# Bounds check for empty places, and one score product for two heads, in a transformer block with mixture of experts

## Chip, cores and metric

The kernel runs on one core of a Trainium2 chip. The metric is device time in microseconds. Three runs of the kernel before gave 1973.52, 1975.29 and 1976.34 us; their median is 1975.29 us.

## What is computed

Sixteen sequences of 512 tokens with 256 features pass a block in fp32. First comes windowed attention: 16 heads of 16 features, windows of 64 queries, which see the band of the 64 keys up to their own. It is mixed by a gate with a linear state-space scan, and an MLP (256 to 1024 to 256) follows. Then each token goes to the two best of 8 experts. The core of the reference:

```python
scores = jnp.einsum('bhncd,bhnkd->bhnck', Qb, Kw) / np.sqrt(Dh)
p = jax.nn.softmax(jnp.where(mask, scores, -jnp.inf), axis=-1)
o = jnp.einsum('bhnck,bhnkd->bhncd', p, Vw)
...
x = x + g * attn + (1.0 - g) * y_ssm
x = x + jax.nn.gelu(h @ mlp_W1 + mlp_b1, approximate=False) @ mlp_W2 + mlp_b2
...
weights, sel = jax.lax.top_k(xf @ gate_w, k=2)
y = experts(xf)                     # swiglu, 8 experts, 256 -> 512 -> 256
out = (take(y, sel) * softmax(weights)).sum()
x = x + gb * out
```

## The kernel before

**Two stages.** Stage one handles a sequence ("batch") at a time: `front` (layer norms, products for q, k and v, scan, gate), `attention` (four tiles of 128 queries), `back` (MLP) and `route` (choice of experts). Stage two, `experts`, handles tiles of 256 places, each of one expert: 64 whole tiles, then 3 half tiles of 128 places.

**The order.** Each part is a generator that yields due times, in units of a batch. The constants in lines 38 to 69 hold them (for example `SCORES`, `VALUES`, `TURNS` for attention and `FULL` for the experts). The loop at the end (lines 1189 to 1194) always advances the part that is due first, and `InOrder` (line 182) makes each engine keep the order in which instructions were written. So batches overlap, and the first expert tiles overlap with the last batch. A different constant moves an instruction on its engine's queue.

**Scores.** A product contracts over 32 partitions, which hold two heads of 16 features. To keep the two apart, `front` (lines 611 to 626) stores q twice, with the features of one head of each pair set to zero by the factors `par`. It copies from PSUM with DVE into copy 0 and with ACT into copy 1; k is copied once, by ACT. `scores` (line 681) then makes 32 products for 128 queries: 2 feature halves, 2 copies, 2 windows, 4 row groups, each 64 queries by 128 keys. In the trace each product is two matmul instructions, so 64 for a tile. `masked`, `numerators` and `turn` add the mask, take the exponent and transpose; `values` (line 732) multiplies by v, in two halves (`chunk`) of 16 products into the PSUM tile `po`.

**Places.** `route` gives each of a token's two choices a row in the DRAM table `place_d`: the token's number and its weight. `place` (line 892) writes 128 rows with an indirect DMA from POOL; a small memset of `between` separates two writes in a row. Each expert has `CAP` rows. Rows that get no token have weight zero, but still need a row of the output to which a tile's scatter-add can add zero, and which no other place of that tile writes. So the table gives them numbers of tokens that did not choose this expert: `others` (line 906) works these out from batch 0, and `fill` (line 924) writes them with 32 more indirect DMAs, from due time 3.5 on, one every 6 us of due time.

**An expert tile.** `places_of` (line 264) loads the tile's rows and also the rows one tile before (`mt`, two blocks). `gather` (line 280) casts the token numbers (`gi`), gathers the tokens from `h_d` (`hr`), and works out the output row `si` on POOL: the tile's own token where the weight is positive, else the other block's. `turned`, `hidden` and `combine` transpose, run the expert, and add the result to the output by an indirect DMA that accumulates. A scatter-add waits until both of the previous tile's have landed, and the cast into a buffer of `si` waits until the scatter-add that last used it has landed.

Of the kernel before, what the change touches and what calls it, by code (L numbers as in the profile page):

```python
# [8 lines left out]
F32 = mybir.dt.float32  # L9
# [28 lines left out]
FRONT = (-1.4961, -1.0671)  # L38
XT = -0.6
QK = (-0.5602, -0.4769, -0.4522, -0.3053)  # L40
V = (-0.0188, 0.0729)
DRIVE = 0.1154
GATE = (-0.0778, 0.205)
BACK = (1.1529, 1.2977)
UP = (
    (1.4542, 1.4907, 1.5377, 1.6049),
    (1.6857, 1.7521, 1.7795, 1.9017),
)
GELU = (1.6239, 2.022)
DOWN = (  # L50
    (1.7436, 1.7759, 1.8584, 2.12),
    (2.1788, 2.1889, 2.2678, 2.288),
)
ROUTE = 2.3576
RATE = 0.01396

LOGITS_GAP = -1.6691
TOKENS_GAP = 1.9608

FULL = (15.9711, 16.4769, 16.5285, 16.7838, 0.0292)  # L60

SCORES = -0.9527
MASKED = (-0.9009, -0.6206)
NUMERATORS = (-0.5391, -0.2136)
NUMERATORS_EACH = 0.1267
TURNS = (0.3291, 0.6595)
OVER_SUMS = 0.8221
VALUES = (1.1056, 1.1201)
MIX = 1.5924
# [6 lines left out]
CAP = TS + TOKENS  # L76
# [8 lines left out]
NROW = NE * CAP + (NE + 1) * TS  # L85
# [3 lines left out]
def block_kernel(  # L89
# [72 lines left out]
    for e in range(NE):  # L162
        nc.gpsimd.memset(rev[:, :, e], float(NE - e))
        nc.gpsimd.memset(first_place[:, :, e], float(e * CAP + TS))

# [8 lines left out]

    idle = w.tile([P, NE + 1, 2, 2], F32, name="idle")
    nc.vector.memset(idle, 0.0)
    nc.gpsimd.iota(
        idle[:, :, :, 0], pattern=[[0, NE + 1], [1, 2]], base=0, channel_multiplier=2,
        allow_small_or_imprecise_dtypes=True,
    )  # L180

# [82 lines left out]
    def places_of(room, j):  # L264

        n = parts(j)
        r = register(room["rows"](j), NROW - 2 * n * P)
        mt = room["mt"]([P, 2, n, 2], F32, name=f"mt_{j}")
        last_load[:] = [
            nc.sync.dma_start(  # L270
                out=mt,
                in_=place_d[bass.ds(r, 2 * n * P), :].rearrange("(q p h) c -> p q h c", p=P, h=n),
            )
        ]
        if j in (0, FIRST):
            for put in placed:
                tc.add_manual_dep(last_load[0].ins, put.ins.name, landed)
        return mt

    def gather(room, j, mt):  # L280

        before, mt = mt[:, 0], mt[:, 1]
# [137 lines left out]
    with ExitStack() as p1, ExitStack() as p2:  # L420
# [17 lines left out]
        cT_sb = load(cT, "cT_sb")  # L438
# [28 lines left out]
        sc = w1p.tile([P, KC, NB], F32, name="sc")  # L467
# [22 lines left out]
        for half in range(2):  # L490
# [30 lines left out]
        prefill += [  # L521
            nc.sync.dma_start(
                out=place_d[: NE * CAP, :].rearrange("(p r) c -> p (r c)", p=P),
                in_=v_cross.rearrange("p t h e -> p (t h e)")[:, : NE * CAP * 2 // P],
            ),
            nc.sync.dma_start(
                out=place_d[NE * CAP :, :].rearrange("(q p h) c -> p q h c", p=P, h=2), in_=idle
            ),
        ]
# [52 lines left out]
        def front(b, t):  # L582
# [28 lines left out]
            t["q"] = q = sb.tile([P, 2, KC, SEQ], F32, tag="q", name=f"q_{b}")  # L611
            t["k"] = kT = sb.tile([P, KC, WIN + SEQ], F32, tag="k", name=f"k_{b}")
            gpsimd.memset(kT[:, :, 0:WIN], 0.0)
            for c in range(2 * KC):
# [66 lines left out]
        def scores(b, t, qt):  # L681
# [6 lines left out]
            for c in range(KC):  # L688
                for e in range(2):
                    for half in range(2):  # L690
                        n = 2 * qt + half
                        for j in range(4):
                            rs = slice(32 * j, 32 * j + 32)
                            tensor.matmul(
                                sc[j // 2][half * WIN : (half + 1) * WIN, j % 2, 2 * c + e, :],
                                q[rs, e, c, n * WIN : (n + 1) * WIN],
                                kT[rs, c, n * WIN : (n + 2) * WIN],
                                start=True, stop=True,
                            )
# [192 lines left out]
        def place(row, at, **kwargs):  # L892

            if placed and gpsimd.last is placed[-1]:
# [3 lines left out]
                in_=row, in_offset=None, **kwargs,  # L898
            )
            for zeros in prefill:  # L900
                tc.add_manual_dep(put.ins, zeros.ins.name, landed)
# [3 lines left out]

        def others(both, pr):

            far = float(NROW)
            nr = few.tile([P, NT, NE], F32, tag="nr", bufs=1, name="nr")
            vector.tensor_sub(nr, tok0[:, :NT].unsqueeze(2).to_broadcast([P, NT, NE]), pr)  # L910

            over = few.tile([P, NT, NE], F32, tag="over", bufs=1, name="over")
            vector.tensor_single_scalar(over, nr, float(TS), ALU.is_ge)
            vector.tensor_max(over, over, both)
            vector.tensor_add(nr, nr, first_place)
            vector.scalar_tensor_tensor(nr, over, far, nr, ALU.mult, ALU.add)
            ni = few.tile([P, NT, NE], I32, tag="ni", bufs=1, name="ni")
            vector.tensor_scalar_add(ni, nr, -float(TS))
            none = few.tile([P, NT, 2], F32, tag="none", bufs=1, name="none")
            gpsimd.memset(none, 0.0)  # L920
            gpsimd.tensor_copy(none[:, :, 0], tok0[:, :NT])
            spare.update(none=none, ni=ni)

        def fill(b, t):

            for e in range(NE):
                for i in range(NT):
                    place(
                        spare["none"][:, i, :], spare["ni"][:, i, e : e + 1],
                        bounds_check=NROW - 1, oob_is_err=False,  # L930
                    )
                    yield 6.0

        def route(b, t):
# [77 lines left out]
            if b == 0:  # L1012
                others(both, pr)
# [73 lines left out]
        def last_table():  # L1087

            assert len(routed) == NB and len(placed) == NT * (NE + 2 * NB)
# [12 lines left out]
            vector.tensor_scalar(start[:, :1], whole[:, :1], float(TS), float(P), ALU.mult, ALU.add)  # L1102
# [26 lines left out]
        def experts(_, t):  # L1129
# [5 lines left out]
            assert len(placed) >= NT * (NE + 2 * done)  # L1135
# [23 lines left out]
            for kind, bufs in (  # L1159
                ("w1", 3), ("w2", 3), ("b1", 3), ("b2", 3), ("mt", FIRST + 4), ("gi", 5),  # L1160
                ("real", 5), ("so", 5), ("si", 5), ("hr", 5), ("hT2", 2), ("act", 2), ("g2", 2),
# [17 lines left out]
        spare = {}  # L1179
# [88 lines left out]
```

## Time and profile before

| | |
|---|---|
| runs, median of 3 | 1975.29 us |
| profiled execution | 1981.67 us |
| its span, first to last instruction | 1979.9 us |
| mean granted clock of TensorE | 0.986 |
| busy PE / weight loads / DVE / ACT / POOL | 95% / 78% / 72% / 49% / 61% |
| score products (`sc`) | 4096 instructions, 81.6 us busy |
| products with v (`po`) | 4096 instructions, 111 us busy |
| scatter-adds (`out<-y,si`) | 131, 1685 ns each on POOL |
| place writes / fill writes | 128 / 32, 1035 / 1040 ns each on POOL |

PE is TensorE's matmul queue, PEld its weight loads, which overlap the matmuls, DVE is VectorE, ACT ScalarE, POOL GpSimd, SP SyncE. Most instructions show line 190, the wrapper `InOrder`, so groups are read by the names of their tiles. Stage one lasts until about 1170 us and stage two until the end, with an overlap of some 150 us. The profiled execution is one run, and stands 6.4 us over the median.

### The profile page before, as it was taken

How to read it: one execution, taken by the hardware profiler on the slowest of the kernel's cores; microseconds unless marked ns; L12 is line 12 of the kernel's file. 1: busy time of each engine (PE TensorE's matmuls, PEld its weight loads, DVE VectorE, ACT ScalarE, POOL GpSimd, SP SyncE). 2: the span in 40 equal slices, each digit the busy share in tenths (PEclk: the TensorE clock that was granted, in tenths of full speed). 3: DMA queues.
4: the chain of work that ended last, by engine and by line, in shares of the span. 5: the costliest groups of instructions: out<-in, count | busy, mean ns of one | idle time of the engine just before them, and what ended most of it. 6: DMA issues, size and time to landing. Idle time of an engine off the chain costs nothing.

```text
span 1979.9 us, 45068 instructions
## 1 busy us (share of the span) xinstructions
PE 1877.9 (95%) x16802; PEld 1543.0 (78%) x16802; DVE 1426.1 (72%) x3243; ACT 975.9 (49%) x2880; POOL 1202.8 (61%) x1869
## 2 busy tenths in 40 slices
PE   5889999989999999999999987989999999999996
PEld 2668877767778778877877776878888888888885
DVE  6778888778889888888888764556665656566664
ACT  2877776766777777787777652111111111111110
POOL 2326558667558547646655555757676666666653
PEclk9999999999999999999999998999999999999998
DMA  5202222212222212223122127578887877878774
GB/s 159 79 25 57 66 52 58 66 52 58 60 58 58 71 47 73 55 57 76 52 50 52 42 57 195 139 192 235 230 237 228 241 223 233 238 225 244 222 227 113
DMA packets 148098, 242.76 MB, mean 123 GB/s; under 512 B 46000, under 2 KB 112432, under 8 KB 139040
## 3 DMA queue, kind: packets, MB, share of 16 engines
q1 hardware_dynamic: 113120, 187.32, 32.8%
q0 software_dynamic: 34464, 51.69, 10.9%
q8 instruction: 134, 2.20, 0.5%
q14 instruction: 92, 0.75, 0.2%
q10 hardware_dynamic: 288, 0.79, 0.1%
HBM read 190.27 MB, written 43.19 MB: 118 GB/s over the span
## 4 chain that ended last, share of the span: by engine, by line
PE 73%; ACT 7%; POOL 6%; DVE 6%; issue 4%; DMA 2%; SPq 0%; POOLq 0%; DVEq 0%; ACTq 0%
PE pgv L190 21%; PE pye L190 11%; PE py L190 9%; PE pmlp L190 7%; PE po L190 4%; PE pq L190 4%; PE pp L190 4%; PE sc L190 2%; PE pa L190 2%; ACT sm L190 2%; DMA out<-y,si 2%; PE pv L190 2%; PE pg L190 2%; ACT L190 2%; POOL h L190 2%
## 5 line engine op out<-in xcount | busy, mean ns | idle before, releaser
L190 PE MATMUL pgv<-hT,we 128*128 128x256 f32 (+1 forms) x2144 | 469.1, 377 | 2.9 <-ACT hT L190 2.9
L190 PEld LDWEIGHTS pgv<-hT,we 128*128 128x128 f32 x2144 | 402.9, 192 | 57.6 <-ACT hT L190 3.7
L190 ACT ACTIVATE sm<-sm,nm 128x128 f32<-128x128 f32 x1024 | 399.1, 394 | 3.7 <-DVE nm L190 3.3
L190 DVE TENSOR_SCALAR gv<-pgv,be 128x256 f32<-128x256 f32 (+1 forms) x536 | 230.9, 473 | 182.1 <-PE pgv L190 145.6
L190 ACT ACTIVATE gv<-gv 128x512 f32<-128x512 f32 (+1 forms) x134 | 83.1, 620 | 455.1 <-DVE gv L190 433.3
L190 POOL DMA_INDIRECT out<-y,si x131 | 220.8, 1685 | 109.4 <-DVE y L190 70.1
L190 PE MATMUL pye<-we,act 128*128 128x256 f32 x1048 | 249.8, 382 | 0.5 <-DVE act L190 0.5
L190 PE MATMUL pmlp<-hT,mw_sb 128*128 128x256 f32 x1024 | 246.2, 385 | 0.4 <-ACT hT L190 0.4
L190 PE MATMUL py<-mw_sb,m 128*128 128x256 f32 x1024 | 236.9, 382 | 0.1
L190 PEld LDWEIGHTS pmlp<-hT,mw_sb 128*128 128x128 f32 x1024 | 190.5, 192 | 37.5 <-issue 9.8
L190 PEld LDWEIGHTS pye<-we,act 128*128 128x128 f32 x1048 | 195.3, 192 | 24.9 <-DVE act L190 0.9
L190 PEld LDWEIGHTS py<-mw_sb,m 128*128 128x128 f32 x1024 | 189.8, 190 | 28.5 <-issue 3.2
L190 ACT ACTIVATION_READ_ACCUMULATOR sm<-sm,nm 128x1 f32 x1024 | 195.8, 191 | 0.0
L190 POOL DMA_INDIRECT place_d<-pl,slot x128 | 132.5, 1035 | 100.6 <-DVE pick L190 71.8
L190 POOL TENSOR_TENSOR e<-e,g 128x256 f32<-128x256 f32 x64 | 47.5, 742 | 221.7 <-DVE e L190 221.7
L190 DVE TENSOR_TENSOR sm<-sc,mask 128x1024 f32<-128x1024 f32 x128 | 155.1, 1212 | 16.7 <-PE sc L190 13.2
L190 DVE TENSOR_REDUCE nm<-sm 128x8 f32<-128x1024 f32 x128 | 156.2, 1220 | 4.4
L190 POOL DMA_INDIRECT hr<-h_d,gi x131 | 134.5, 1027 | 38.5 <-issue 19.5
L190 ACT COPY pT<-pp 128x1024 f32<-128x1024 f32 x128 | 128.9, 1007 | 32.3 <-PE pp L190 28.8
L190 PE MATMUL pp<-ident,sm 128*128 128x128 f32 x1024 | 134.8, 275 | 6.9 <-DVE sm L190 6.9
L190 DVE TENSOR_SCALAR m<-pmlp,b_sb 128x256 f32<-128x256 f32 x256 | 109.7, 470 | 40.2 <-PE pmlp L190 38.3
L190 PEld LDWEIGHTS pp<-ident,sm 128*128 128x128 f32 x1024 | 119.3, 143 | 16.1 <-issue 5.7
(219 smaller groups left out, 3217.1 us busy)
## 6 DMA issues: line engine op xcount, KB each, us to landing
we<-in_e_w SPq DMA_DIRECT2D x67, 1024.0 KB
we<-in_e_w SPq DMA_DIRECT2D x67, 512.0 KB
v_cross<-v_own SPq DMA_DIRECT2D x48, 256.0 KB
be<-in_e_b SPq DMA_DIRECT2D x67, 128.0 KB
x<-in_x SPq DMA_DIRECT2D x16, 512.0 KB
xr<-in_x SPq DMA_DIRECT2D x32, 256.0 KB
out<-h SPq DMA_DIRECT2D x16, 512.0 KB
h_d<-hn SPq DMA_DIRECT2D x16, 512.0 KB
```

The source lines that it names most:

```text
L190: put = getattr(self.engine, name)(*args, **kwargs)
```

## The change

Two edits, and new due times.

Places without a token: a place's row is now just token number and weight, and an empty row is all zeros. In `gather` an empty place's output row gets the number of tokens (`TOKENS`) added, so it lies beyond the end of the output, and the scatter-add has a bounds check that drops such rows. `others`, `fill`, `idle` and the second block of `mt` are gone; the table has no spare block ahead of each expert.

Scores: q is stored once, k twice (copy 0 by DVE, copy 1 by ACT). One product now has the 128 keys of both copies side by side, so 16 products of 64 by 256 replace 32 of 64 by 128.

The due times are all new. On the engines' queues this puts the first half of each tile's products with v (16 of `po`) ahead of the scores two tiles on, where before only one tile of four was so split, `pq_3` one MLP product earlier, and in the overlap of the stages the first `prank` ahead of the first expert tile's transpose, and the last batch's `ahead` on POOL behind a scatter-add of tile 2 (before: behind the index casts and scatter-adds of later tiles).

```diff
-SCORES = -0.9527
-MASKED = (-0.9009, -0.6206)
...
-VALUES = (1.1056, 1.1201)
+SCORES = -0.9284
+MASKED = (-0.9272, -0.6892)
...
+VALUES = (1.0622, 1.1426)
-FULL = (15.9711, 16.4769, 16.5285, 16.7838, 0.0292)
+FULL = (15.9709, 16.4684, 16.5007, 17.0256, 0.0287)
...
-CAP = TS + TOKENS
+CAP = TOKENS
-NROW = NE * CAP + (NE + 1) * TS
+NROW = NE * CAP + NE * TS
...
-        mt = room["mt"]([P, 2, n, 2], F32, name=f"mt_{j}")
+        mt = room["mt"]([P, n, 2], F32, name=f"mt_{j}")
...
-        real = room["real"]([P, n], F32, name=f"real_{j}")
-        gpsimd.tensor_single_scalar(real, mt[:, :, 1], 0.0, ALU.is_gt)
+        si = room["si"]([P, n], I32, name=f"si_{j}")
         so = room["so"]([P, n], F32, name=f"so_{j}")
-        gpsimd.tensor_sub(so, mt[:, :, 0], before[:, :, 0])
-        gpsimd.tensor_mul(so, so, real)
-        si = room["si"]([P, n], I32, name=f"si_{j}")
-        gpsimd.tensor_add(so, so, before[:, :, 0])
+        gpsimd.tensor_scalar(so, mt[:, :, 1], 0.0, float(TOKENS), ALU.is_le, ALU.mult)
+        gpsimd.tensor_add(so, so, mt[:, :, 0])
         gpsimd.tensor_copy(si, so)
...
             in_=y, in_offset=None, compute_op=ALU.add,
+            bounds_check=room["tokens"](j) - 1, oob_is_err=False,
...
                 if c < KC:
-                    vector.tensor_scalar_mul(q[:, 0, c, :], pq, par[:, 0:1])
-                    scalar.activation(q[:, 1, c, :], pq, AF.Identity, scale=par[:, 1:2])
+                    scalar.copy(q[:, c, :], pq)
                 else:
-                    scalar.copy(kT[:, c - KC, WIN:], pq)
+                    vector.tensor_scalar_mul(kT[:, c - KC, 0, WIN:], pq, par[:, 0:1])
+                    scalar.activation(
+                        kT[:, c - KC, 1, WIN:], pq, AF.Identity, scale=par[:, 1:2]
+                    )
...
-                for e in range(2):
-                    for half in range(2):
...
-                                sc[j // 2][half * WIN : (half + 1) * WIN, j % 2, 2 * c + e, :],
-                                q[rs, e, c, n * WIN : (n + 1) * WIN],
-                                kT[rs, c, n * WIN : (n + 2) * WIN],
...
+                            sc[j // 2][
+                                half * WIN : (half + 1) * WIN, j % 2, 2 * c : 2 * c + 2, :
+                            ],
+                            q[rs, c, n * WIN : (n + 1) * WIN],
+                            kT[rs, c, :, n * WIN : (n + 2) * WIN],
...
-        def others(both, pr):
-        def fill(b, t):
...
-            if b == 0:
-                others(both, pr)
...
-            (3.5, -1, places(fill(0, {}), 0, 3.5)),
```

More of the change, by code (lines that the diff above doesn't have):

```diff
@@ L34 @@
 NEG = -1.0e30
[L38 to L44, printed above, removed]
+FRONT = (-1.4781, -1.0684)
+XT = -0.6004
+QK = (-0.5706, -0.4649, -0.4626, -0.324)
+V = (-0.0324, 0.0643)
+DRIVE = 0.1113
+GATE = (-0.004, 0.2002)
+BACK = (1.1554, 1.3131)
 UP = (
-    (1.4542, 1.4907, 1.5377, 1.6049),
-    (1.6857, 1.7521, 1.7795, 1.9017),
+    (1.4542, 1.4907, 1.5377, 1.6035),
+    (1.6843, 1.7508, 1.7782, 1.9466),
 )
-GELU = (1.6239, 2.022)
+GELU = (1.6378, 2.0259)
 DOWN = (
-    (1.7436, 1.7759, 1.8584, 2.12),
-    (2.1788, 2.1889, 2.2678, 2.288),
+    (1.7089, 1.8492, 1.8707, 2.1323),
+    (2.1911, 2.2012, 2.2773, 2.2985),
 )
-ROUTE = 2.3576
+ROUTE = 2.3589
 RATE = 0.01396
-LOGITS_GAP = -1.6691
-TOKENS_GAP = 1.9608
-FULL = (15.9711, 16.4769, 16.5285, 16.7838, 0.0292)
-SCORES = -0.9527
-MASKED = (-0.9009, -0.6206)
[L64 to L67, printed above, removed]
-VALUES = (1.1056, 1.1201)
-MIX = 1.5924
+LOGITS_GAP = -1.9886
+TOKENS_GAP = 1.9209
+FULL = (15.9709, 16.4684, 16.5007, 17.0256, 0.0287)
+SCORES = -0.9284
+MASKED = (-0.9272, -0.6892)
+NUMERATORS = (-0.5869, -0.2654)
+NUMERATORS_EACH = 0.1497
+TURNS = (0.4019, 0.6275)
+OVER_SUMS = 0.8312
+VALUES = (1.0622, 1.1426)
+MIX = 1.5922
 TS = 256
@@ L163, in block_kernel @@
         nc.gpsimd.memset(rev[:, :, e], float(NE - e))
-        nc.gpsimd.memset(first_place[:, :, e], float(e * CAP + TS))
+        nc.gpsimd.memset(first_place[:, :, e], float(e * CAP))
     taken = w.tile([P, NE + 1], F32, name="taken")
@@ L173, in block_kernel @@
     nc.vector.memset(gate_sb, 0.0)
[L175 to L180, printed above, removed]
     class InOrder:
@@ L266, in places_of @@
         n = parts(j)
-        r = register(room["rows"](j), NROW - 2 * n * P)
-        mt = room["mt"]([P, 2, n, 2], F32, name=f"mt_{j}")
+        r = register(room["rows"](j), NROW - n * P)
+        mt = room["mt"]([P, n, 2], F32, name=f"mt_{j}")
         last_load[:] = [
@@ L271, in places_of @@
                 out=mt,
-                in_=place_d[bass.ds(r, 2 * n * P), :].rearrange("(q p h) c -> p q h c", p=P, h=n),
+                in_=place_d[bass.ds(r, n * P), :].rearrange("(p h) c -> p h c", h=n),
             )
@@ L280, in gather @@
     def gather(room, j, mt):
-        before, mt = mt[:, 0], mt[:, 1]
         n = parts(j)
@@ L435, in load @@
             return t
-        cT_sb = load(cT, "cT_sb")
+        cT_sb = sb.tile(list(cT.shape), F32, tag="e", bufs=1, name="cT_sb")
+        nc.sync.dma_start(out=cT_sb, in_=cT)
         wm = [
@@ L463, in block_kernel @@
         mw2_sb = w2p.tile(list(mw2.shape), F32, name="mw2_sb")
-        sc = w1p.tile([P, KC, NB], F32, name="sc")
+        sc = sb.tile([P, KC, NB], F32, tag="oT", name="sc")
         nc.scalar.activation(sc, cT_sb, AF.Tanh, scale=0.5)
@@ L520, in block_kernel @@
         nc.gpsimd.memset(v_cross, 0.0)
-        prefill += [
+        prefill.append(
             nc.sync.dma_start(
[L523 to L529, printed above, removed]
+                out=place_d.rearrange("(p r) c -> p (r c)", p=P),
+                in_=v_cross.rearrange("p t h e -> p (t h e)")[:, : NROW * 2 // P],
+            )
+        )
         par = w1p.tile([P, 2], F32, name="par")
@@ L609, in front @@
             yield from to_features(xn, xnT, 0, 0, b)
-            t["q"] = q = sb.tile([P, 2, KC, SEQ], F32, tag="q", name=f"q_{b}")
-            t["k"] = kT = sb.tile([P, KC, WIN + SEQ], F32, tag="k", name=f"k_{b}")
-            gpsimd.memset(kT[:, :, 0:WIN], 0.0)
+            t["q"] = q = sb.tile([P, KC, SEQ], F32, tag="q", name=f"q_{b}")
+            t["k"] = kT = sb.tile([P, KC, 2, WIN + SEQ], F32, tag="k", name=f"k_{b}")
+            gpsimd.memset(kT[:, :, :, 0:WIN], 0.0)
             for c in range(2 * KC):
@@ L622, in front @@
                 if c < KC:
-                    vector.tensor_scalar_mul(q[:, 0, c, :], pq, par[:, 0:1])
-                    scalar.activation(q[:, 1, c, :], pq, AF.Identity, scale=par[:, 1:2])
-                else:
-                    scalar.copy(kT[:, c - KC, WIN:], pq)
+                    scalar.copy(q[:, c, :], pq)
+                else:
+                    vector.tensor_scalar_mul(kT[:, c - KC, 0, WIN:], pq, par[:, 0:1])
+                    scalar.activation(
+                        kT[:, c - KC, 1, WIN:], pq, AF.Identity, scale=par[:, 1:2]
+                    )
             for i in range(0, NT, 2):
@@ L688, in scores @@
             for c in range(KC):
-                for e in range(2):
-                    for half in range(2):
[L691 to L694, printed above, removed]
-                                sc[j // 2][half * WIN : (half + 1) * WIN, j % 2, 2 * c + e, :],
-                                q[rs, e, c, n * WIN : (n + 1) * WIN],
-                                kT[rs, c, n * WIN : (n + 2) * WIN],
-                                start=True, stop=True,
-                            )
+                for half in range(2):
+                    n = 2 * qt + half
+                    for j in range(4):
+                        rs = slice(32 * j, 32 * j + 32)
+                        tensor.matmul(
+                            sc[j // 2][
[3 more added lines that the diff above has]
+                            kT[rs, c, :, n * WIN : (n + 2) * WIN],
+                            start=True, stop=True,
+                        )
             return sc
@@ L890, in one_hot, with place @@
             return mx, oh
-        def place(row, at, **kwargs):
+        def place(row, at):
             if placed and gpsimd.last is placed[-1]:
@@ L897, in place @@
                 out=place_d, out_offset=bass.IndirectOffsetOnAxis(ap=at, axis=0),
-                in_=row, in_offset=None, **kwargs,
+                in_=row, in_offset=None,
             )
-            for zeros in prefill:
-                tc.add_manual_dep(put.ins, zeros.ins.name, landed)
+            tc.add_manual_dep(put.ins, prefill[0].ins.name, landed)
             if placed:
@@ L904, in place @@
             placed.append(put)
-        def others(both, pr):
[L908 to L922, printed above, removed]
-        def fill(b, t):
[L926 to L932, printed above, removed]
         def route(b, t):
@@ L1087, in last_table @@
         def last_table():
-            assert len(routed) == NB and len(placed) == NT * (NE + 2 * NB)
+            assert len(routed) == NB and len(placed) == NT * 2 * NB
             one = room["one"]
@@ L1101, in last_table @@
             start = one.tile([P, 2], F32, name="start")
-            vector.tensor_scalar(start[:, :1], whole[:, :1], float(TS), float(P), ALU.mult, ALU.add)
+            vector.tensor_scalar_mul(start[:, :1], whole[:, :1], float(TS))
             steps_h = one.tile([P, NE], F32, name="steps_h")
@@ L1134, in experts @@
             yield (FULL[1],)
-            assert len(placed) >= NT * (NE + 2 * done)
+            assert len(placed) >= NT * 2 * done
             top.close()
@@ L1160, in experts @@
                 ("w1", 3), ("w2", 3), ("b1", 3), ("b2", 3), ("mt", FIRST + 4), ("gi", 5),
-                ("real", 5), ("so", 5), ("si", 5), ("hr", 5), ("hT2", 2), ("act", 2), ("g2", 2),
+                ("so", 5), ("si", 5), ("hr", 5), ("hT2", 2), ("act", 2), ("g2", 2),
                 ("v2", 2), ("y", 4),
@@ L1177, in experts @@
                 yield (FULL[3] + FULL[4] * piece,)
-        spare = {}
         queue = [
             (XT - 0.01, -2, places(modulation(0, {}), 0, XT - 0.01)),
-            (3.5, -1, places(fill(0, {}), 0, 3.5)),
             (FULL[0], -2, places(experts(0, {}), 0, FULL[0])),
```

## The prediction

> **What bounds it now.** I read the busy row and its slices first: TensorE (PE) is busy 95% of the span, and 9 tenths or more in most slices. The gaps are at the start, in slices 6 to 10, in 23 to 26 and at the end. Then busy time by stretch, cut where each batch's query products start on the chain. Columns: length, then busy PE, weight loads, DVE, ACT, POOL with counts, clock, DMA share, GB/s.
>
> ```profile
> 267.40:343.41 76.01, 72.36 (x833) 56.88 (x833) 60.86 (x140) 53.18 (x167) 54.95 (x79) 1.00 0.25 57
> 343.41:419.37 75.96, 72.33 (x833) 56.88 (x833) 60.97 (x140) 53.31 (x167) 56.34 (x80) 1.00 0.22 57
> 419.37:497.33 77.96, 73.12 (x833) 57.21 (x833) 60.88 (x140) 53.07 (x167) 53.02 (x77) 1.00 0.21 56
> 568.39:639.37 70.98, 70.48 (x834) 56.44 (x834) 61.03 (x140) 53.13 (x168) 43.59 (x62) 1.00 0.27 61
> ```
>
> The same work takes 70.98 us in the last row, where PE idles 0.5 us, and 76 to 78 in three earlier batches, where POOL has 9 to 13 us more to do. The chain that ended last shows why (columns: start, length, engine, tile):
>
> ```profile
> 388.01 1.00 POOL place_d L190
> 390.75 1.00 POOL place_d L190
> 392.05 1.34 POOL place_d L190
> 393.40 1.07 POOL rs_b L190
> 394.66 1.16 POOL place_d L190
> 399.94 1.00 POOL place_d L190
> 401.24 0.99 POOL place_d L190
> 402.24 1.08 POOL rs_c L190
> 403.35 3.08 DVE xn L190 x4
> ```
>
> POOL's index writes stand in line ahead of rs_b and rs_c, and the layer norm's DVE work waits for those. From 1347 us to 1953 us PE is busy without a gap (expert tiles, about 10.8 us each). Between 1134 and 1347 us PE idles some 30 us (busy time by stretch), the first 130 us idle 35, and the last 20 are scatter-adds landing in turn.
>
> **The fill goes.** 32 indirect writes of idle places, 272 to 471 us:
>
> ```profile
> L190 POOL DMA_INDIRECT place_d<-none,ni x32: 973/1010/1351, 272.0 to 471.3; - x32
> L190 POOL DMA_INDIRECT place_d<-pl,slot x128: 959/999/1491, 222.4 to 1342.7; - x128
> ```
>
> (min/median/max ns.) 32 x 1.04 = 33.3 us of POOL, in exactly the three long batches. With them gone these have the POOL work of the others, and what ends last is PE, as there: 76.01 + 75.96 + 77.96 - 3 x 70.98 = **-17.0 us**. Bounds: 0, if the order of the early batches is slow for another reason, and -17.6, if the 71.63 us of the batch before counts too. I take -17: the excess starts and ends with the fill. The DVE work of `others` (about ten operations, 0.2 us each, once) lies under PE.
>
> **Scores.** From the timeline of PE in a steady batch (start, length with the last result's drain, form):
>
> ```profile
> 638.17 1.21 PE L190 MATMUL sc<-k,q 32*64 32x128 f32 x64
> 639.30 1.98 PE L190 MATMUL pq<-xnT,wqkv_sb 128*128 128x512 f32 x4
> 641.22 0.43 PE L190 MATMUL po<-pT,v_cross 128*32 128x64 f32 x16
> 647.72 1.89 PE L190 MATMUL pmlp<-hT,mw_sb 128*128 128x256 f32 x8
> 658.17 1.50 PE L190 MATMUL sc<-k,q 32*64 32x128 f32 x64
> 659.60 0.43 PE L190 MATMUL po<-pT,v_cross 128*32 128x64 f32 x16
> ```
>
> Start to next start, 64 score products take 1.13 us, or 1.43 where they wait 0.3 us for the second k copy. A 128-column product of the whole array takes 109 ns (8 pp in 0.87), a 256-column one 216 ns (8 pmlp in 1.73). In the trace's single starts the 64 come in groups of eight, the groups 109 ns apart: eight products run side by side, and streaming, not issue, sets the pace; only the last 32 drift, by some 0.08 us. So 32 products of 256 columns need 32/8 x 216 = 0.86 us where 64 of 128 need 64/8 x 109 = 0.87. Half the instructions buy the drift alone: 0.08 us in three bursts of a batch, and with the stall 0.37 in the fourth, if k comes in time: pq_3 now stands one MLP product earlier and a burst of po ahead of the scores. Together -0.61 us a batch.
>
> The page "TensorE: Matmul & The Clock Gate" of the Trainium skill, "Back-to-back" issue, says that start to start never drops below about 25 ns. This trace has 17.7 ns on average and about 7 inside a group, so the floor doesn't hold for packed tiles here; by it a burst would go from 1.6 to about 0.86 us, and the change would gain some 47 us.
>
> Against this stands the new order: the due times put half of each tile's po products ahead of the scores, where three tiles of four had all 64 together. One more entry into po per tile: entering po costs 0.2 us (4 pq take 4 x 0.43 = 1.72 of the 1.92 us to the next start), entering sc 0.1 (8 pmlp take 1.73 of 1.82, seen before the burst at 658.17). Extra po entry 0.2, one more end of a po burst 0.14, less the sc entry 0.1: +0.24 in three tiles, +0.10 in the fourth (already split), +0.82 a batch. Net +0.21, over the 14 batches that PE bounds: **+3 us**. Bounds: -9 (14 x -0.61, the order free) and, if the wide products overlap only four deep, 32/4 x 216 = 1.73 + 0.26 of entry and drain = 1.99 for 1.21 on average: 0.78 x 64 = 50, and the order's 11: +61. I take +3, since the grouping of eight is in the rows.
>
> **q and k.** Before, q had a DVE (710 ns) and an ACT copy (681), k an ACT copy (577), twice each; now q has one, k two. Same sum per engine. The zeroing of k doubles (206 ns, at most 412) on a POOL that idles 27 us a batch. 0, bounds -1 to +3.
>
> **Gather and scatter of the experts.** Six small POOL operations per tile become four: 274+235+418+224+193 = 1344 ns behind the first cast become about 274+224+193 = 691, so -0.65 us in 67 tiles. In the steady stretch POOL is busy 65 to 68 of 100 us: hidden. The bounds check of the scatter-add has no row. The fill's writes have one and cost 1010 ns against 999 without; the other end is the 650 ns by which a scatter-add (1685 ns) tops a plain write (1035): 2 x 0.65 = 1.3 us a tile, still under POOL's 3.5 us of slack a tile, but 9 scatters between 1244 and 1310 us and 3 at the end are exposed: 12 x 0.65 = +8. Rows that are dropped, and half the bytes of mt, give at most 2 back. I take 0.
>
> **Between the stages.** PE's largest stalls there are these two; each rank product waits for POOL's `ahead`:
>
> ```profile
> 1219.33 0.64 PE L190 MATMUL prank<-ahead,ones 128*128 128x32 f32 x2 [5.32 <-POOL ahead L190]
> 1308.56 0.64 PE L190 MATMUL prank<-ahead,ones 128*128 128x32 f32 x2 [5.85 <-POOL ahead L190]
> ```
>
> In the new order the first comes before tile 0's transpose and product, which now run after the wait: 0.44 + 1.73 = +2.2, less 2 x 0.65 of POOL in front: +0.9. At the second, `ahead` stands behind the first scatter of tile 2, not behind an index cast that waits for landings, and PE has some 7 us of product in between: -5.9. Sum -5; with the experts' start due 0.24 batch later I take **-4**, bounds -15 and +10 (half and a third of the 30 us idle).
>
> **Start and end.** In the first 130 us the scores now stand behind a po burst (16 in 0.24, so 0.6 us with entry); both wait for the same pT, so two to four such delays of 0.6 on the chain: **+1**, bounds 0 and +3. The end stays.
>
> **Sum:** -17 + 3 - 4 + 1 = -17 us on the profiled execution, 1981.7 us (span 1979.9): 1964.7. That one lies 6.4 us over the median of the runs, 1975.3; so **1958**.
>
> **Rivals.**
> - *The order costs nothing* and stalls between the stages shrink: -17 - 9 - 10 = -36, 1939. For it: batches now idle only 0.5 us, so entries are the only price. Against: the entries are in the rows. 0.10.
> - *Given back:* entries and late DVE copies cost 1 us a batch, +14 for +3: about 1970 to 1974. For it: DVE's second k copy stands behind the routing's chain of small operations, which waits for ACT's exponent. Against: k is needed some 6 us after pq_3. 0.10.
> - *Slower: the wide products lose overlap.* +61 for +3: 2016. It decides from +0.33 us a burst over the forecast (21/64), that is bursts of 1.4 us or more. For it: both heads of a pair now share a longer product per tile, and no row has 256 columns in small tiles. Against: the same eight tiles and PSUM banks are in use before. 0.08.
> - *Slower: the check isn't free,* or the change doesn't free the early batches: +8 for 0 and 0 for -17: up to 1983. 0.04.
>
> **Chances.** The forecast with its own range, 1946 to 1970, has 0.68. Reaching into the rivals to 1940 and 1976 adds about 0.06 each: 0.80. A measurement tells about 0.2%, 4 us, from no change. Faster 0.80, within it 0.08, slower 0.12.
>
> **What would show it.** Batches between 270 and 500 us at about 71 us and no place_d ahead of rs_c on the chain; score bursts of 32 at about 1.06 us; steady batches at 71.0 to 71.4; only one prank wait over 5 us; scatter-adds still near 1.6 us. I am wrong if steady batches pass 72 us, if score bursts pass 1.4 us, or if the long early batches stay.

## The result and the profile after

The changed kernel takes **1959.24 us** (median of 6 runs, 1957.57 to 1959.92), the kernel before in the same set 1974.07 us (6 runs): a ratio of **0.9923 [0.991, 0.9935]**. A second set gave 1959.22 us and 0.9917 [0.9904, 0.9931]. The profiled execution after took 1959.1 us (span 1957.4), close to its median, while that of before stood 7.6 us over its own. The forecast was 1958. The time is right, but several of its terms were not, and their errors cancel.

Busy time by stretch, for the batches that the fill had made long before (same columns as in the prediction):

```profile
266.27:337.74 71.47, 70.86 (x706) 55.40 (x706) 61.84 (x140) 52.81 (x168) 43.95 (x61) 1.00 0.22 60
337.74:409.20 71.46, 70.86 (x706) 55.39 (x706) 61.83 (x140) 52.79 (x168) 43.93 (x61) 1.00 0.29 61
409.20:480.67 71.47, 70.86 (x706) 55.40 (x706) 61.63 (x140) 52.81 (x168) 43.92 (x61) 1.00 0.23 60
```

POOL's extra 9 to 13 us are gone, and from the fourth on all batches are alike. But they are 0.49 us longer than the 70.98 of before, and PE idles 0.6 us in each. The chain that ended last shows with what (start, length, engine, tile):

```profile
388.08 1.88 POOL rs_b L182
390.16 1.15 POOL place_d L182
...
397.41 1.05 POOL rs_c L182
398.49 3.10 DVE xn L182 x4
401.59 1.15 DVE sm L182
402.75 1.22 DVE nm L182
404.36 1.56 PE pa L182 x6
```

Every steady batch now runs for a while through POOL and DVE: the layer norm's `rs_c` on POOL, then on DVE `xn`, `sm`, `nm` and, left out of this list, `oT`, for which the mixing product `pa` waits. In the steady batch of before the chain stayed on PE at this place.

The timeline of PE in a steady batch:

```profile
768.28 1.89 PE L182 MATMUL pmlp<-hT,mw_sb 128*128 128x256 f32 x8
770.10 0.43 PE L182 MATMUL po<-pT,v_cross 128*32 128x64 f32 x16
770.35 0.41 PE L182 MATMUL po<-pT,v_own 128*32 128x64 f32 x16
770.69 1.12 PE L182 MATMUL sc<-k,q 32*64 32x256 f32 x32
771.74 1.98 PE L182 MATMUL pq<-xnT,wqkv_sb 128*128 128x512 f32 x4
```

From 770.69 to 771.74 is 1.05 us for 32 wide products (forecast 1.06), in all four bursts of a batch. Ahead of them stands the first half of `po`, as the diff of the due times said.

Between the stages, the two rank products that had waited 5.32 and 5.85 us:

```profile
1196.20 0.41 PE L182 MATMUL prank<-ahead,ones 128*128 128x32 f32 x2 [2.04 <-POOL ahead L182]
1273.43 0.41 PE L182 MATMUL prank<-ahead,ones 128*128 128x32 f32 x2 [0.37 <-POOL ahead L182]
```

**How to read the runs.** The profiles are compared piece by piece, cut at instructions that all of them have: the fourth batch's first `pq`, the last batch's first `pq`, and the first `pgv` of the 15th expert tile. All in us; the median of the timed runs stands last.

| kernel | to 4th batch | 12 batches | between the stages | rest | span | median |
|---|---|---|---|---|---|---|
| before | 191.0 | 869.5 | 340.4 | 579.0 | 1979.9 | 1974.07 |
| e5 (before + check) | 191.8 | 864.4 | 335.9 | 580.0 | 1972.1 | 1973.22 |
| after | 194.8 | 857.6 | 326.5 | 578.5 | 1957.4 | 1959.24 |
| e1 (places alone) | 191.2 | 851.8 | 341.3 | 578.6 | 1962.9 | 1967.39 |
| e2 (both, old times) | 194.2 | 860.3 | 340.1 | 578.7 | 1973.3 | 1975.70 |
| e3 (after, narrow) | 194.1 | 874.4 | 334.4 | 578.2 | 1981.1 | 1981.17 |
| e4 (fill spread) | 192.7 | 866.1 | 342.7 | 579.9 | 1981.4 | 1981.04 |
| e6 (after, old FULL) | 194.5 | 857.6 | 336.2 | 577.3 | 1965.6 | 1969.53 |
| e7 (e1, new FULL) | 190.7 | 851.8 | 335.5 | 579.1 | 1957.1 | 1962.79 |
| e8 (both, old times, pq_3, new FULL) | 194.1 | 851.0 | 336.6 | 578.1 | 1959.8 | 1964.22 |
| e9 (e7, table earlier) | 191.3 | 851.9 | 325.4 | 578.7 | 1947.3 | 1950.96 |
| e10 (e8, table and pq_3 earlier) | 196.3 | 860.2 | 326.0 | 578.6 | 1961.1 | 1964.50 |
| e11 (after again) | 193.7 | 857.5 | 328.3 | 578.7 | 1958.2 | 1959.22 |
| e12 (e8, table earlier) | 195.0 | 850.8 | 324.1 | 578.4 | 1948.3 | 1950.01 |

In the set of e1 to e4 the kernel before itself had a median of 1986.04 us (1981.94 to 1991.51), in the others 1971.83 to 1974.81; so ratios of that set are not put beside ratios of another, and the pieces are read instead. The pieces need care too: in the profiles of before and of e1 to e4 PE pauses beside some of POOL's indirect writes with no semaphore behind it, and in the other nine it never does (last section). In e1 and e2 all of these pauses, 2 us of idle PE, lie between the stages; in before, e3 and e4 most lie in the 12 batches.

### The profile page after: what moved, and what is told of

Same layout as the page of the kernel before. It is cut to its first block, busy times and chain, and to the rows that moved or that the text cites. A ratio compares the mean times of both kernels' runs of the same rounds, so it can differ in the third digit from the quotient of the medians.

```text
span 1957.4 us, 40907 instructions
## 1 busy us (share of the span) xinstructions
PE 1875.3 (96%) x14754; PEld 1522.2 (78%) x14754; DVE 1432.1 (73%) x3236; ACT 972.3 (50%) x2880; POOL 1146.3 (59%) x1684
## 4 chain that ended last, share of the span: by engine, by line
PE 73%; DVE 11%; POOL 8%; issue 4%; ACT 2%; DMA 2%; SPq 0%; POOLq 0%; DVEq 0%; ACTq 0%
PE pgv L182 22%; PE pye L182 11%; PE pmlp L182 10%; PE py L182 6%; PE pq L182 5%; PE po L182 4%; PE pa L182 3%; PE pp L182 3%; PE pv L182 2%; PE sc L182 2%; DVE xn L182 2%; DVE sm L182 2%; DVE nm L182 2%; POOL h L182 2%; DMA out<-y,si 1%
## 5 line engine op out<-in xcount | busy, mean ns | idle before, releaser
L182 POOL DMA_INDIRECT out<-y,si x131 | 219.0, 1672 | 120.9 <-DVE y L182 85.6
```

The lines of the kernel that those rows point to most:

```text
L182: put = getattr(self.engine, name)(*args, **kwargs)
```

## The experiments

**e1, places alone.** The diff's edits to places and gather, with narrow scores and all of before's due times.

> Only the places' edit (no fill, empty places dropped by the bounds check), with the old narrow score products and the old due times. My theory: the fill alone cost 17.0 us in three batches, the check is free; so -17 to -18 us against the kernel before, about 1957, all batches between 200 and 1065 us at 70.98 us, and PE's stalls between the stages (prank 5.3 and 5.9 us) as before. Rival A (the fill only filled POOL's idle time, and the early batches were long because of their order): they stay at 76 us and the time at 1974. Rival B (the check on the scatter-add costs POOL time): scatter-adds longer than 1685 ns, 1962 or more.

Measured: 1967.39 us, 0.9906 [0.9891, 0.9922] in its set. All 12 batches take 70.98 us. So the fill alone made the early batches long. The theory holds there, and the two waits of `prank` stay (5.4 and 5.9 us). The stretch between the stages is 341.3 us, the longest but one: 340.4 in before and 335.9 in e5. But the pauses lengthen it in e1 and in before, and e5 has none, so whether the places' edit gives something back there is not shown.

**e2, both edits at the old due times.** The changed kernel with lines 38 to 69 of before (except `CAP`).

> The changed kernel with all due times of the kernel before: wide score products, no fill, old order (64 products with v together in three tiles of four). My theory: the batch of 71.47 us is the new order's doing, and the wide products gain 0.08 us in each burst; so 70.4 to 70.8 us a batch, and with the old stalls between the stages 1950 to 1956 us. Rival (the wide products, or the second k copy, make the batch longer): batches stay near 71.5 us, 1963 to 1966.

Measured: 1975.70 us, 0.995 [0.9937, 0.9964]; steady batches 71.74 us. My theory fell. The rival's batches held (near 71.5 us), its time (1963 to 1966) did not, in a set in which before itself ran 12 us longer. The timeline of all engines at the second score burst:

```profile
791.10 0.69 PE L182 MATMUL sc<-k,q 32*64 32x256 f32 x16
791.31 0.74 DVE L182 TENSOR_SCALAR k<-pq,par 128x512 f32<-128x512 f32 x1
792.09 0.69 ACT L182 ACTIVATE k<-pq,par 128x512 f32<-128x512 f32 x1 [0.71 <-DVE k L182]
...
792.83 0.69 PE L182 MATMUL sc<-k,q 32*64 32x256 f32 x16 [1.05 <-ACT k L182]
```

The two copies of k do not run side by side: ACT, idle for 0.71 us, waits for DVE's copy, and the burst waits 1.05 us for ACT's. k is complete 1.47 us after the first copy starts, where one ACT copy took 0.57 before. The page "PSUM — Partial Sum Buffer" of the Trainium skill, "PSUM bank collisions raise a hardware error", says that two engines may not touch one bank at once, not even to read; both copies read the same PSUM tile, and the trace agrees in the order: ACT waits for DVE's copy and starts 0.04 us after it ends. The reason for that wait the trace doesn't show.

**e3, the changed kernel with narrow scores.** Old `scores` loop and q and k copies, new due times.

> The changed kernel with the old narrow score products and the old q and k copies, but its new due times. My theory: the order costs some 0.8 us a batch and the wide products save 0.08 to 0.1 us a burst, so batches of 71.8 to 72.0 us, and 1963 to 1967 us. Rival (the wide products are what made the batch longer): 70.98 us a batch and 1952.

Measured: 1981.17 us, 0.9974 [0.9963, 0.9985]; batches 72.85 us, a microsecond over what the theory had. PE and POOL in the third tile's scores (timeline of all engines):

```profile
812.75 0.41 PE L182 MATMUL po<-pT,v_own 128*32 128x64 f32 x16
813.09 1.47 PE L182 MATMUL sc<-k,q 32*64 32x128 f32 x50
...
813.54 0.99 POOL L182 DMA_INDIRECT place_d<-pl,slot  x1 [0.15 <-issue]
814.86 0.55 PE L182 MATMUL sc<-k,q 32*64 32x128 f32 x14 [0.30 <-issue]
```

and the same place in the changed kernel:

```profile
802.43 1.12 PE L182 MATMUL sc<-k,q 32*64 32x256 f32 x32
802.89 0.99 POOL L182 DMA_INDIRECT place_d<-pl,slot  x1 [0.15 <-issue]
803.48 0.70 PE L182 MATMUL py<-mw_sb,m 128*128 128x256 f32 x2
```

In both, one of the routing's own index writes starts on POOL 0.46 us into the burst. From there the 64 narrow products stall (first to last start 2.04 to 2.10 us in 11 batches of 11, and 0.94 in the other three bursts), with no semaphore behind it: the releaser is "issue". The 32 wide ones take 0.74 us in 11 of 11. Without that 1.15 us a batch e3 would be at 71.7 (an estimate), 0.1 under what the theory had. So the excess is not a semaphore wait, but a pause beside an indirect DMA. That the wide products are spared is not shown: the two profiles come from different sets, and the changed kernel's has no pause anywhere. In e5, which has none either, 64 narrow products beside a place write (at 250 us) take their 0.94 us, and 1.54 in before.

**e4, the fill spread out.** In before, `yield 6.0` in `fill` becomes `yield 25.0`: the same 32 writes, over 11 batches.

> The kernel before with one change: a fill write is due every 25 us of due time, not 6, so that its 32 writes fall on eleven batches, three in each. My theory: it was their density, 11 writes of 1.04 us ahead of the layer norms' POOL work in one batch, that made a batch long, and POOL idles 27 us of an ordinary batch; three writes a batch then cost 0 to 0.5 us each batch, and the time is 1957 to 1963. Rival (each write on POOL costs its 0.5 us wherever it stands): 1974.

Measured: 1981.04 us, 0.9973 [0.9964, 0.9983]. Batches vary from 70.98 to 73.25 us; the sum, 866.1, is hardly below that of before. The theory's time fell. The rival's price is near: some 14.2 us over 12 batches of 70.98 are 0.44 us a write. But the reason is not POOL's line: 13.0 of the 14.2 us are in the starts of `sc` and `po`, and the other 1.2 are waits for DVE's `sm`, `oT` and `xn` in one batch. In the longest (73.25 against 70.98) the starts of `sc` and `po` take 1.33 and 0.93 us more, the whole excess, and both stalls, with releaser "issue", begin while POOL makes a fill write. It is e3's effect, and e4 was timed in the same set. What the spread fill costs in an execution without pauses no run shows, so the theory is not tested.

**e5, the bounds check alone.** Before, with one line more in `combine`:

```diff
+            bounds_check=room["tokens"](j) - 1, oob_is_err=False,
```

> The kernel before, with the bounds check on its scatter-adds and nothing else; the fill stays, so no row is dropped. Theory (the check is free): ratio 1.000, within 0.2%, and scatter-adds at 1.67 to 1.70 us of POOL as before (1685 ns). Rival (the check costs up to 0.65 us for a scatter-add): scatter-adds at 2.0 us or more, 4 to 8 us slower.

Measured: 1973.22 us, 0.9992 [0.9983, 1.0001]. A scatter-add takes 1684 ns on POOL with the check, 1685 without. The check is free where it drops nothing; in the changed kernel, where it drops the empty places, a scatter-add takes 1672 ns. As a profile, e5 is a second execution of before: the same instructions but for the check, and 7.8 us shorter.

**e6, the changed kernel with the old `FULL`.**

> The changed kernel with the due times of the experts (FULL) of before, all else as changed. Theory (the 14 us that the stretch from the last batch's first query product to the 14th expert tile is shorter in the changed kernel come from these due times, which set where rank products, index casts and first scatter-adds stand): that stretch goes from 326.5 back to about 340 us, with two prank waits over 5 us, and the time rises by 12 to 15 us; batches stay at 71.47. Rival (they come from the places' edit, which takes index work off POOL, and from the other due times): the stretch stays under 331 us, and the time within 4 us of the changed kernel.

Measured: 1969.53 us, 0.9978 [0.9969, 0.9987], 10.3 us slower than the changed kernel; stretch 336.2 us, prank waits 10.9 and 5.6. The theory holds, with a smaller size.

**e7, places alone with the new `FULL`.**

> The places' edit alone (narrow score products, due times of before within a batch) with the changed kernel's due times for the experts (FULL). Theory (batches at 70.98 us as with the places' edit alone, and the shorter stretch between the stages belongs to FULL): stretch 327 to 331 us instead of 341, 10 to 14 us faster than the places' edit alone, a ratio to before of 0.983 to 0.986, so faster than the changed kernel by 4 to 8 us. Rival (the stretch needs the other due times or the wide products too): the ratio stays at 0.990, within 4 us of the places' edit alone.

Measured: 1962.79 us, 0.9945 [0.9932, 0.9958], stretch 335.5 us. Neither forecast held: its stretch is 5.8 us shorter than e1's, half of what I expected, and part of that are e1's pauses; e5, with the old `FULL`, has 335.9. POOL's timeline ahead of the first rank product:

```profile
1185.41 0.18 POOL L182 CAST gi<-mt 128x2 int32<-128x2 f32 x1 [7.81 <-DMA mt<-place_d]
...
1191.10 0.18 POOL L182 CAST gi<-mt 128x2 int32<-128x2 f32 x1 [1.88 <-DMA mt<-place_d]
...
1195.37 0.76 POOL L182 TENSOR_TENSOR ahead<-ahead,both 128x8 f32<-128x8 f32 x3
```

The casts into `gi` wait for the expert tables `mt`, `ahead` stands behind them, and the first `prank` waits 12.81 us for it. Why `mt` is late shows on SP's queue:

```profile
1159.48 0.37 SPq L262 DMA_DIRECT2D mt<-place_d  x1
1160.68 0.37 SPq L237 DMA_DIRECT2D we<-in_e_w  x1
1163.80 0.41 SPq L909 DMA_DIRECT2D out<-h  x1
...
1172.42 0.38 SPq L903 DMA_DIRECT2D h_d<-hn  x1
...
1174.82 0.34 SPq L262 DMA_DIRECT2D mt<-place_d  x1
...
1183.61 11.49 SPq L262 DMA_DIRECT2D mt<-place_d  x10
```

All loads of tables but the first are queued behind two stores of stage one, and `h_d<-hn` must wait for the batch's own end. So the tables come at a time that the end of stage one sets.

**e8, both edits, old order in the batch, pq_3 one MLP product earlier, new `FULL`.**

```diff
-QK = (-0.5602, -0.4769, -0.4522, -0.3053)
+QK = (-0.5602, -0.4769, -0.4522, -0.324)
```

> The changed kernel (both edits) with the due times of before, except that pq_3 stands one MLP product earlier and the experts' due times (FULL) are the changed ones. Theory (with the old due times the wide products lost 1.05 us a batch only because the second half of the second tile's scores waited for k, and the po bursts stay together): all four score bursts 1.05 us, no k wait, batches at 70.4 to 70.5 us, stretch between the stages 327 to 331 us, a ratio of 0.979 to 0.983. Rival (the second k copy moves another wait into the batch, as the changed order shows with its 0.7 us ahead of pa): batches at 71.0 us or more, a ratio of 0.986 or more.

Measured: 1964.22 us, 0.9952 [0.994, 0.9965]; batches 70.95, stretch 336.6. The theory fell: the burst still waits 0.3 us for ACT's k, and pieces of a burst that stops pay its end twice, so the four bursts take 4.72 us instead of 4.20; and the stretch is that of e7.

**e9, e7 with the tables 0.03 batch earlier.**

```diff
-FULL = (15.9709, 16.4684, 16.5007, 17.0256, 0.0287)
+FULL = (15.9709, 16.4384, 16.5007, 17.0256, 0.0287)
```

> As e7 (places' edit alone, FULL of the changed kernel), but the second of the experts' due times is 0.03 batch earlier (16.4384 for 16.4684), so that on SP the loads of mt_1 to mt_11 stand ahead of the stores h_d<-hn and out<-h of batch 13 or 14, as they do in the changed kernel, and not behind them. Theory (in e7 the 10 us that the batches had saved were lost because POOL's casts into gi waited 7.8 and 1.9 us for mt, and ahead and prank behind them, 12.8 us): no cast waits for mt, the first prank waits 1 to 4 us, and the time falls by 7 to 11 us against e7, to a ratio of 0.989 to 0.991. Rival (the wait moves to something else that is not ready earlier, the weights, the gathered rows or the last batch's route): within 4 us of e7, with the largest PE wait under another name.

Measured: **1950.96 us**, 0.9882 [0.9867, 0.9897], 11.8 us faster than e7. SP's queue now has all the loads ahead of the store:

```profile
1159.80 0.37 SPq L262 DMA_DIRECT2D mt<-place_d  x1
...
1163.70 0.34 SPq L262 DMA_DIRECT2D mt<-place_d  x1
...
1167.50 10.47 SPq L262 DMA_DIRECT2D mt<-place_d  x10
1178.07 0.39 SPq L903 DMA_DIRECT2D h_d<-hn  x1
```

and the first rank product on PE waits 2.74 us:

```profile
1186.79 0.64 PE L182 MATMUL prank<-ahead,ones 128*128 128x32 f32 x2 [2.74 <-POOL ahead L182]
```

No cast waits for `mt` any more. The stretch is 325.4 us, 10.1 less than in e7, and the wait of `prank` is 10.07 us less: the theory holds (9.8 us by span, and by the medians a little past its range). This kernel has no wide scores, and it beats both kernels.

**e10, e8 with the tables earlier and pq_3 at -0.4.**

> As e8 (both edits, due times of before within a batch), with the experts' table loads early on SP as in e9, and pq_3 due at -0.4 instead of -0.324, so another MLP product earlier. Theory (the 0.5 us a batch that e8 still loses at the scores is k coming late, and the loads of mt hold up the start of the experts): batches at 70.4 to 70.5 us, all score bursts 1.05 us, first prank wait 1 to 4 us, a ratio of 0.984 to 0.988, faster than the changed kernel by 8 to 15 us. Rival (the loop of POOL and DVE work from rs_b to oT, which ends the changed kernel's batches, is next in line): batches at 70.8 us or more; or the stretch between the stages gives the rest back: ratio 0.990 or more.

Measured: 1964.50 us, 0.9954 [0.994, 0.9967]. The tables do what they did in e9 (326.0), but batches are 71.69 us: with pq_3 so early ACT's exponents come later, and the second score burst now waits 0.6 us for ACT's `pT`. The theory for the batch fell. The rival's bounds are met, but the wait is not the one that it named.

**e11, the changed kernel again.**

> The changed kernel once more, on the chip of e9 and e10. Theory (most of the 5 us by which the profiled execution of before stood over its median was the length of the fill's batches and of the stretch between the stages, which differ from run to run; the changed kernel has no fill): batches again at 71.46 to 71.47 us from the fourth on, span within 3 us of 1957.4, ratio 0.991 to 0.9935. Rival (its batches differ from run to run too): a spread of 1 us or more among the steady batches, or a span over 1961.

Measured: 1959.22 us, 0.9917 [0.9904, 0.9931]; span 1958.2, batches 71.45 to 71.47. The theory holds. The stretch between the stages is 328.3 us, 1.8 more than in the first profile, and the second `prank` waits 2.61 us there.

**e12, e8 with the tables earlier.** Only `FULL` as in e9.

> As e8 (both edits, due times of before within a batch, pq_3 due at -0.324), with only the second of the experts' due times 0.03 batch earlier, as in e9. Theory (the early loads of mt are worth as much here as between e7 and e9, some 10 us, and the wide products nothing: batches at 70.95 us against 70.98, and some 2 us more in the first four batches): a ratio of 0.988 to 0.991, within 4 us of e9. Rival (the wide products are worth something once the batches and the experts' start are in order): a ratio under 0.986.

Measured: 1950.01 us, 0.9888 [0.9872, 0.9905]; batches 70.95, stretch 324.1. The theory holds: wide scores and narrow ones (e9) are the same in time, as far as these runs tell; the way to the 4th batch is 3.7 us longer, where I had 2. The changed kernel is 9.1 us of span behind e12: 6.8 in its 12 batches, which are 0.5 to 0.7 us longer each in its new order, and 2.4 between the stages.

## Why the prediction was right, and where it was not

Against e5, the execution that stands at its median, the change comes to +3.0 (to the 4th batch) - 6.8 (12 batches) - 9.4 (between the stages) - 1.5 (rest) = -14.7 us; 1974.07 - 14.7 = 1959.4, measured 1959.24. The rest of 1.5 us is within what executions differ by there (577.3 to 580.0).

That 1958 came so close is luck. For the profiled execution the forecast was 1964.7, and the changed kernel's took 1959.1. Only because another 6.4 us were taken off does the median agree: the stretch between the stages gained 5 us more than forecast, and this paid for the fill, the order and the start, each of which came out dearer than forecast.

- **The fill, -17.** Mechanism right (e1: every batch at 70.98), size right for the execution that I read, too large for a typical one. In e5 the 12 batches exceed e1's by 864.4 - 851.8 = 12.6 us, in the profile of before by 17.7. Some 4.3 us of that difference of 5.1 are pauses that I had not looked at: PE's waits in its three fill batches show `po` held up by "issue" for 1.1, 1.1 and 2.1 us, beside fill writes. The timeline of all engines in before:

```profile
441.05 0.32 PE L190 MATMUL po<-pT,v_own 128*32 128x64 f32 x3 [0.41 <-issue]
441.11 0.98 POOL L190 DMA_INDIRECT place_d<-none,ni  x1 [0.18 <-issue]
441.79 0.32 PE L190 MATMUL po<-pT,v_own 128*32 128x64 f32 x4 [0.42 <-issue]
...
442.39 0.98 POOL L190 DMA_INDIRECT place_d<-none,ni  x1 [0.19 <-issue]
442.52 0.28 PE L190 MATMUL po<-pT,v_own 128*32 128x64 f32 x3 [0.41 <-issue]
```

  In e5 the same writes stand beside the same products, and none pauses. So "1964.7, less 6.4" was a wrong step: the 6.4 us that the profiled execution lay over the median sat in the batches whose excess the change removes (5.1 us against e5) and between the stages (4.5), and I took the former off twice.
- **Scores, -0.61 a batch.** Right: 4.20 us in four bursts against 4.84, -0.64. The floor of 25 ns from start to start, weighed in the prediction, would have made some 47 us of it; the bursts deny that.
- **The new order, +0.82 a batch.** Its sum was mis-sized and its kind only half right: from start to start `po` takes 0.41 us more, half of my entries; `prank` and `py` take 0.09 more each, `pmlp` and `pg` as much less. Another 0.72 stands ahead of and in `pa`, the wait for DVE's `oT` behind `xn`, `sm` and `nm`: 0.41 + 0.72 - 0.64 = +0.49. I had priced PE's entries and not looked at what DVE's new order makes late. Net +0.49 for +0.21, over 12 batches +5.9.
- **q and k copies, 0.** Right within the steady batch of the changed kernel, where pq_3 is early enough; k is complete some 0.9 us before the second half of the burst starts. But the price was read as a sum per engine, and the two copies come one after the other: 1.05 us a batch under the old times (e2).
- **Gather, scatter, check, 0.** Right (e5). The rival of a dear check is out.
- **Between the stages, -4.** This step failed. It was -9.4 against e5 (-7.6 in e11) and -13.9 against the profile of before. The second prank went as worked out (5.85 to 0.37, forecast -5.9), though in e11 it waits 2.61. The first was to be late by +0.9 and came down from 5.32 to 2.04, because the tables were there. Rows of SP and POOL in the profile before had said so; SP's second load of `mt` and ten more stand behind the store `h_d<-hn`, and a cast waits for them (10.0 us in all):

```profile
1195.68 0.38 SPq L945 DMA_DIRECT2D h_d<-hn  x1
...
1198.07 0.40 SPq L270 DMA_DIRECT2D mt<-place_d  x1
...
1206.96 11.06 SPq L270 DMA_DIRECT2D mt<-place_d  x10
...
1209.44 0.18 POOL L190 CAST gi<-mt 128x2 int32<-128x2 f32 x1 [9.78 <-DMA mt<-place_d]
```

  In the changed kernel all these loads come first, and no cast waits for them:

```profile
1176.47 11.15 SPq L262 DMA_DIRECT2D mt<-place_d  x10
1187.73 0.39 SPq L907 DMA_DIRECT2D h_d<-hn  x1
```

  I named POOL's queue and PE's, and did not follow SP's, on which `FULL` moved the loads ahead of the store. e6 and e9 show it from both sides. A faster clock is no rival: PE's busy time in this stretch is 305.6 us in e6 and 305.5 in the changed kernel, so the difference is idle time.
- **Start, +1.** Mis-sized: +3.0 (+1.9 in e11). Where the chain has no cover, k's second copy costs 0.9 us at once (PE's waits in the first 600 us: `sc` for ACT's k, 0.9), and the second batch is 2 us longer both with the new order alone (e3, 55.9 against 53.9) and with the wide products alone (e2, 55.6). But in e4, which has before's instructions up to there, it is 55.4, so this part is not shown to be the change's.
- **Rivals.** The wide products did not lose overlap. "Given back" was right in kind for the order, a wait on DVE, not in size.

Whether the change helps is a question of its two halves: the places' edit takes 12.6 us off the batches (e1 against e5) and saves nothing that shows between the stages; moving the tables is worth some 10 us there (e7 to e9 by span, e6 to the changed kernel); the wide scores are worth nothing that the runs can tell (e9, e12), and the new order within the batch, with them, costs some 6 us (857.6 against e1's 851.8).

## What to carry to other kernels

Before a profiled execution's distance to the median is taken off a sum, find the stretch in which it lies: if the change removes that stretch, the distance goes with it. A look for waits of PE on "issue" and a second profile tell whether the first one is a typical execution. When due times move work, follow every queue that they reorder, the DMA issuing one first: eleven loads of 2 KB behind one store that waits cost some 10 us, and halving the number of score instructions brought nothing that shows in the time (e12 against e9). And cost a split copy by when its last part lands, not by busy time.

## What was not expected of the hardware

While POOL makes an indirect DMA, bursts of TensorE products can pause for 0.3 to 0.7 us at a time, from start to start, with no semaphore behind it. Whether they do seems to be a matter of the execution more than of the kernel, though no kernel was profiled both with and without them. Products with v beside a place write near the end of stage one, on PE and POOL, in e1:

```profile
1085.47 1.00 POOL L182 DMA_INDIRECT place_d<-pl,slot  x1 [0.15 <-issue]
1085.58 0.29 PE L182 MATMUL po<-pT,v_own 128*32 128x64 f32 x7
1086.06 0.31 PE L182 MATMUL po<-pT,v_own 128*32 128x64 f32 x4 [0.18 <-issue]
1086.79 0.34 PE L182 MATMUL po<-pT,v_own 128*32 128x64 f32 x5 [0.43 <-issue]
```

and the same products beside the same write in e7:

```profile
1084.94 0.99 POOL L182 DMA_INDIRECT place_d<-pl,slot  x1 [0.15 <-issue]
1085.05 0.44 PE L182 MATMUL po<-pT,v_own 128*32 128x64 f32 x16
```

In both the write starts 0.58 us into a burst of 64 products, which takes 2.02 us in e1 and 0.92 in e7. Of the 14 profiles those of before and of e1 to e4 have such pauses, and the other nine have none. Over 11 batches, e3's 64-product bursts took 2.04 to 2.10 us beside a write that starts 0.46 us in, and 0.94 without one; in e4 bursts beside fill writes took up to 2.13. A write that starts 1.1 us ahead of the burst, and so ends as the burst starts, did not hurt (0.94, 11 of 11 in e1). Wide score bursts beside a write (0.74) were profiled only in executions without pauses, so whether longer products are spared is not shown; in e3 one product of 256 columns (`pgv`) waits 0.8 us on "issue" beside two writes. e1 to e4 were timed in the one set in which before took 1986 us. It fits that this whole set ran with pauses, but no profile of before was taken in it.

The page "Runtime: NRT & Kernel Launch" of the Trainium skill, "Instruction fetch mechanics", says that fetching the instruction stream is mostly hidden; whether these pauses are late instructions no run here shows. In e3 the 16 KB transfers of the queue that the profile calls "instruction" (q8) start at any distance from the pause, from 2.5 us before its end to 3.7 us after it and farther, while the pause comes in 11 batches of 11. That speaks against late transfers of this queue; the cause stays open.
